# Work carried across three stage borders in a four-layer fp32 model on one Trainium2 core

## The chip, the core and the metric

The kernel runs on one core of one Trainium2 chip. A core has five engines with a queue of instructions each, which they work off in order: PE multiplies matrices (its weight loads are shown as PEld), DVE is the vector engine, ACT the scalar engine, POOL the third general engine, and SP only issues transfers. They meet at semaphores. The metric is the device time of one execution in microseconds (us), lower is better.

## The reference, cut to what matters

x is fp32, 16 sequences of 256 rows of 128 features. Four layers follow, each of two sublayers of one form:

```python
x = x + _layernorm(_L0_attn_ref(_layernorm(x), ...))     # causal attention
x = x + _layernorm(_L0_ffn_ref(_layernorm(x), ...))      # gated mlp
x = x + _layernorm(_L1_attn_ref(_layernorm(x), ...))     # a transformer of depth 4
x = x + _layernorm(_L1_ffn_ref(_layernorm(x), ...))      # soft mixture of experts
x = x + _layernorm(_L2_attn_ref(_layernorm(x), ...))     # causal attention
...                                                      # three more sublayers

def _layernorm(x, axis=-1, eps=1e-05):
    m = jnp.mean(x, axis=axis, keepdims=True)
    v = jnp.var(x, axis=axis, keepdims=True)
    return (x - m) / jnp.sqrt(v + eps)
```

The transformer and the soft mixture, whose borders the change touches:

```python
for i in range(DEPTH):                                   # _L1_attn_ref, DEPTH = 4
    x = x + self_attention(layer_norm(x, ln1_g[i], ln1_b[i]), Wq[i], Wk[i], Wv[i], Wo[i], bo[i])
    h = layer_norm(x, ln2_g[i], ln2_b[i])
    x = x + (jax.nn.gelu(h @ W1[i] + b1[i], approximate=False) @ W2[i] + b2[i])

logits = jnp.einsum('bmd,dnp->bmnp', x, phi)             # _L1_ffn_ref, n = 64, p = 32
dispatch = jax.nn.softmax(logits, axis=0)                # over the sequences b
combine = jax.nn.softmax(logits.reshape(bsz, m, n * p), axis=-1).reshape(bsz, m, n, p)
slots = jnp.einsum('bmd,bmnp->bnpd', x, dispatch)
y = jnp.einsum('bnpd,nde->bnpe', slots, W) + b[None, :, None, :]
out = jnp.einsum('bnpd,bmnp->bmd', y, combine)
```

## The kernel before, in words

x lies in on-chip memory as eight groups of four tiles, a tile being 128 rows of 128 features. A group is the unit of nearly all work: one instruction for a 128x512 block or four for its tiles. The stages follow one another, each with its own pools of buffers: L0 (attention and mlp), the transformer (l1a), the soft mixture (l1f), the second attention (l2a), a trunk, and the rest.

A layernorm is split over the engines. `stats` takes four bn_stats and four bn_aggr on DVE (lines 255 and 257), then `rsqrt` does a scale and a pow on POOL (L244, L245); `normed` writes four tiles on DVE (L264). Two functions inside L0 do the same with ACT: a second pair of small POOL operations (L577, L578) makes a bias, and four activations (L583) write the tiles. Before a matmul by features, four PE transposes by the identity (L306) go to a PSUM bank that ACT copies out.

Three stages matter, and the places where they touch.

L0. `group(g)` is a generator; `turns` steps the eight groups through the instruction order in a manual schedule, group g starting at turn 4g. A group ends with y = mlp output (L719), the normalisation of y and its addition to x (L724), and the normalisation of x into z[g], the transformer's input.

Transformer. `stage_l1_attn` first sets up buffers by memsets on POOL (L746, L748), two casts on DVE (L753), then runs 64 steps: in each of the four layers, eight `l1_mix` (attention, one per group) and eight `ffn`, of which up to five are interleaved. Each begins with `l1_norm_T`: stats, normed, transposes, and xT with the layer's gain and bias on ACT (L776). `l1_mix` has the matmuls wq, wk and tok. In the last layer each ffn adds its result to z (L794), normalises it and adds it to x (`residual`), and `fill` writes x to DRAM as xs (L958) and its normed form to mxn (L264), the mixture's input. The order within the pools is left to a scheduler, apart from the manual schedules of L0 and l2a.

Soft mixture. The slots are cut into eight blocks. `logits(n)` makes block n's logits (PE matmuls phi x mxT, copies lg on ACT, maxima mpart on DVE, L1010), `slots(n)` does the dispatch weights (DVE, L1031 to L1048) and the experts, `share(n)` adds the block's part to x: exponentials, transposes, matmuls my x meT, and on DVE x = x * fade + part (L1145). A loop steps share(n), logits(n + 2) and slots(n + 1) in turn. Ahead of it POOL makes a bf16 split of the experts' biases (L990 to L997). In the last block, after every second sequence, `end(g)` divides group g by its sum (L1164 to L1168), normalises it, and adds back the x that was saved in xs (L1170). The share waits for end(g) to be stepped through.

Second attention. `attention_stage` runs `head(0)` up to its fourth step, sets up buffers by POOL memsets (L344, L349), finishes head 0, and then `turns` the other heads and two batches a group; `beside`, which starts at turn 9, is here `l3_decays`, a set of small operations for the later trunk: 20 on DVE in one piece (L1266 and on), then 16 heads, one after another. Matmuls km x qT give the scores, and DVE takes their maximum (at_nm, L440).

Of the kernel before, what the change touches and what calls it, by code (L numbers as in the profile page):

```python
# [199 lines left out]
class Ctx:  # L200
# [61 lines left out]
    def normed(self, out, src, mv, rs):  # L262
        for k in range(NT):
            self.nc.vector.tensor_scalar(  # L264
                out[:, k, :], src[:, k, :], mv[:, k, 0:1], rs[:, k : k + 1], ALU.subtract, ALU.mult
            )

    def norm_to(self, out, src, wait=1):
# [272 lines left out]
        return out  # L541


def stage_l0(k, x, w, wv, wi, z):


    nc, v, gp = k.nc, k.nc.vector, k.nc.gpsimd
# [8 lines left out]
    def constants():  # L556
# [12 lines left out]
        for name in f:  # L569
            v.tensor_scalar(f[name], wi[name], float(np.float32(1.0 / 127.0)), None, ALU.mult)  # L570
            yield

    def stats(src):

        mv, rs = k.stats(src)
        nb = k.t([P, NT], "ln_nb", 6)
        gp.tensor_scalar(nb, mv[:, :, 0], -1.0, None, ALU.mult)  # L577
        gp.tensor_tensor(nb, nb, rs, ALU.mult)  # L578
        return nb, rs

    def normed(out, src, nb, rs):
        for t in range(NT):
            nc.scalar.activation(  # L583
                out[:, t, :], src[:, t, :], AF.Identity, bias=nb[:, t : t + 1], scale=rs[:, t : t + 1]
            )

    def by_feature(src, tag):
        ps = k.transposed_ps(src)
# [57 lines left out]
        v.tensor_tensor(to, ps[:, : 2 * D].rearrange("p (t d) -> p t d", t=2), bc(sm, 2, D), ALU.mult)  # L646

    def group(g):
        nb, rs = stats(x[g])
        yield from idle(2)  # L650
        xn = k.t([P, NT, D], "xn", 2)
        normed(xn, x[g], nb, rs)
        yield
        xT = by_feature(xn, "xT")
        yield
        qk = []
        for name in ("wq", "wk"):
            ps = k.ps("s")
            k.mm(ps[:32, :], w[name], xT)
            t = k.t([32, GT], name + "T", 2)  # L660
            nc.scalar.copy(t, ps[:32, :])
            qk.append(t)
        yield
        s0 = scores(qk, 0)
        ps = k.tokens_ps(xT, wfull)
        val = k.t([P, NT, D], "v", 3)
        nc.scalar.copy(val, ps)
        yield
        got0 = masked(s0)
        s1 = scores(qk, 1)  # L670
        yield
        e0, sm0 = weights(*got0)
        got1 = masked(s1)
        yield
        e1, sm1 = weights(*got1)
        eT0 = weights_T(e0)
        yield
        o0 = product(eT0, val, 0)
        eT1 = weights_T(e1)
        yield  # L680
        o = k.t([P, NT, D], "o", 3)
        divided(o, o0, sm0, 0)
        o1 = product(eT1, val, 1)
        yield
        divided(o, o1, sm1, 1)
        mv, rs = k.stats(o)
        yield from idle(2)
        k.normed(o, o, mv, rs)
        gp.tensor_tensor(x[g], x[g], o, ALU.add)
        yield  # L690
        nb, rs = stats(x[g])
        yield from idle(2)
        xn = k.t([P, NT, D], "xf", 2)
        normed(xn, x[g], nb, rs)
        yield
        xT = by_feature(xn, "xfT")
        yield
        h = k.t([P, 3, GT], "h", 2)
        todo = []
        for cs in ((0, 1), (2,)):  # L700
            for c, u, sg in todo:
                v.tensor_tensor(h[:, c, :], u, sg, ALU.mult)
            todo = []
            for c in cs:
                cols = slice(c * P, (c + 1) * P)
                gt = k.ps("s")
                k.mm(gt, f["gate"][:, cols], xT)
                u = k.ps("s")
                k.mm(u, f["up"][:, cols], xT)
                sg = k.t([P, GT], "sg", 4)  # L710
                nc.scalar.activation(sg, gt, AF.Silu)
                todo.append((c, u, sg))
            yield
        for c, u, sg in todo:
            v.tensor_tensor(h[:, c, :], u, sg, ALU.mult)
        yield
        ps = k.tokens_ps(h, down)
        y = k.t([P, NT, D], "y", 3)
        nc.scalar.copy(y, ps)  # L719
        yield  # L720
        mv, rs = k.stats(y)
        yield from idle(2)
        k.normed(y, y, mv, rs)
        gp.tensor_tensor(x[g], x[g], y, ALU.add)  # L724
        yield
        nb, rs = stats(x[g])
        yield from idle(2)
        normed(z[g], x[g], nb, rs)
        yield

    with k.tc.manual_schedule():
        k.turns([(0, group(0)), (0, constants())] + [(4 * g, group(g)) for g in range(1, NG)])


def stage_l1_attn(k, x, ws, rows, z, then):

    nc = k.nc

# [4 lines left out]
    k.l1_ctx = [k.t([P, 4, 68], f"l1_ctx{i}", 1) for i in range(2)]  # L743
    k.l1_max = [k.t([P, 2, 3, 4, 32], f"l1_max{i}", 1) for i in range(2)]
    for a in k.l1_val + k.l1_lin:
        nc.gpsimd.memset(a, 1.0)  # L746
    for a in k.l1_max + k.l1_ctx:
        nc.gpsimd.memset(a, 0.0)  # L748
    for a in k.l1_ctx:
# [3 lines left out]
        nc.vector.tensor_copy(a, k.c[n])  # L753

    def ffn(i, g):
        yield from l1_ffn(k, z[g], ws[i], rows[f"b2{i}"])
        if i == 3:
            yield
            yield from k.residual(x[g], z[g])
            yield  # L760
            yield from then(g)

    steps, leads = [], []
    for i in range(4):
        steps += [l1_mix(k, z[g], ws[i], rows[f"bo{i}"], NG * i + g) for g in range(NG)]
        steps += [ffn(i, g) for g in range(NG)]
        leads += [4] * NG + [2] * NG
    k.interleave(steps, 5, leads, -1)


# [6 lines left out]
    return out  # L777


def l1_ffn(k, z, w, b2):  # L780

    hT = yield from l1_norm_T(k, z, w["ln2_g"], w["ln2_b"])
    k.nc.gpsimd.tensor_tensor(z, z, bc(b2, 1, NT), ALU.add)
# [7 lines left out]
            yield  # L791
    ps = k.tokens_ps(h, w["w2"].rearrange("p (c n) -> p c n", c=4))
    yield
    k.nc.vector.tensor_tensor(z, ps, z, ALU.add)  # L794


def l1_mix(k, z, w, bo, n):


    nc, v = k.nc, k.nc.vector  # L800
# [1 line left out]
    val, lin, ctx, mx = k.l1_val[n % 3], k.l1_lin[n % 3], k.l1_ctx[n % 2], k.l1_max[n % 2]  # L802
    heads = [slice(32 * h, 32 * h + 32) for h in range(4)]
    tiles = lambda b: [slice((2 * b + t) * P, (2 * b + t + 1) * P) for t in range(2)]
    hT = yield from l1_norm_T(k, z, w["ln1_g"], w["ln1_b"])
    nc.gpsimd.tensor_tensor(z, z, bc(bo, 1, NT), ALU.add)
    yield

# [143 lines left out]
def soft_inputs(k, x, pool):  # L952

    xs = k.dram.tile([P, NG, NT, D], F32, tag="xs", name="xs")
    xn = [pool.tile([P, NT, D], F32, tag=f"mxn{g}", name=f"mxn{g}") for g in range(NG)]

    def fill(g):
        k.nc.sync.dma_start(out=xs[:, g], in_=x[g])  # L958
        yield from k.norm_to(xn[g], x[g])

    return xs, xn, fill


def stage_soft_moe(k, x, w, wdram, bdram, xn, xs):

# [15 lines left out]
    fade, less = {}, {}  # L983
    quarter = k.t([P, P], "mquarter", 1, dt=BF16)
    v.tensor_copy(quarter, w["quarter"])


    bias = k.t([P, 16 * D], "mbias", 1, dt=BF16)
    left = k.t([P, 16 * D], "mdisp", 3)
    nc.gpsimd.memset(left, 0.0)  # L990
    for i in range(3):
        nc.sync.dma_start(out=left[32 * i : 32 * i + 4, :], in_=bdram)
    nc.gpsimd.tensor_copy(bias, left)
    for i in (1, 2):
        for at in (slice(32, 64), slice(64, P))[i - 1 :]:
            nc.gpsimd.tensor_tensor(left[at, :], left[at, :], bias[at, :], ALU.subtract)
            nc.gpsimd.tensor_copy(bias[at, :], left[at, :])  # L997

    def logits(n):
        lg = lgs[n % 2]  # L1000
# [121 lines left out]
    def share(n):  # L1122
# [3 lines left out]
        for b in range(NB):  # L1126
# [15 lines left out]
            for t in range(2):  # L1142
# [3 lines left out]
                else:  # L1146
                    v.tensor_copy(x[g][:, at, :], ps[:, t, 0:D])
            nc.scalar.copy(got[:, :, b], ps[:, :, D])  # L1148
            yield
            if n == blocks - 1 and b % 2:  # L1150
                yield from end(b // 2, f, got)
        if n == 0:
            v.tensor_copy(sums, got)
        elif n < blocks - 1:
# [2 lines left out]

    def end(g, f, got):

        back = k.t([P, NT, D], "slT", 3)  # L1160
        nc.sync.dma_start(out=back, in_=xs[:, g])
        bs = slice(2 * g, 2 * g + 2)
        r = k.t([P, 2, 2], "mend", 2)
        v.tensor_tensor(r, sums[:, :, bs], f[:, :, bs], ALU.mult)  # L1164
        v.tensor_tensor(r, r, got[:, :, bs], ALU.add)
        v.reciprocal(r, r)
        xg = x[g].rearrange("p (b t) d -> p b t d", b=2)
        v.tensor_tensor(xg, xg, bc(r.rearrange("p t b -> p b t"), 3, D), ALU.mult)  # L1168
        n = yield from k.norm(x[g], "mdisp", 3)
        nc.gpsimd.tensor_tensor(x[g], back, n, ALU.add)  # L1170

    for n in range(-2, blocks):
        parts = [
# [1 line left out]
            logits(n + 2) if n + 2 < blocks else None,  # L1175
            slots(n + 1) if 0 <= n + 1 < blocks else None,
        ]
        parts = [p for p in parts if p]
        while parts:
            parts = [p for p in parts if next(p, k) is not k]  # L1180


def stage_l2_attn(k, x, w, beside):

    nc, v = k.nc, k.nc.vector

    def head(g, got):
        yield
        xn = yield from k.norm(x[g], "xn", 1, 2)
        yield  # L1190
        ps = k.transposed_ps(xn)
        xT = k.t([P, GT], "xT", 2)
        nc.scalar.copy(xT, ps)
# [26 lines left out]
        yield  # L1220
        yield from k.residual(x[g], y, 2)

    k.attention_stage(head, 10, 4, tail, beside)


def l2_ffn(k, x, w, b2):
# [598 lines left out]
def program(ctx: ExitStack, tc: tile.TileContext, xin, dram, at, out):  # L1825
# [44 lines left out]
    k.load = load  # L1870
    k.mhalf = base.tile([P, P], F32, tag="mhalf", name="mhalf")
    nc.gpsimd.memset(k.mhalf, -0.5)
    rows1 = load_rows(base, "l1rows")

    @contextmanager
# [12 lines left out]
    k.dram = ctx.enter_context(tc.tile_pool(name="spill", bufs=1, space=bass.MemoryType.DRAM))  # L1888
    pz = opened("z", "left")
    z = [pz.tile([P, NT, D], F32, tag=f"z{g}", name=f"z{g}") for g in range(NG)]  # L1890
    stage("l0", "left", stage_l0, l0, l0v, l0f, z, banks=ONE_RING)
    closed("w0")
    l2 = load(opened("wb", "right"), "l2")
    psoft = opened("soft", "right")
    l1f = load(psoft, "l1f")
    xs, xn, fill = soft_inputs(k, x, psoft)
    stage("l1a", "left", stage_l1_attn, l1, rows1, z, fill, banks=RING_BANKS)
    closed("z")
    closed("wa")

    stage("l1f", "left", stage_soft_moe, l1f, dram["l1fw"], dram["l1fb"], xn, xs)
    closed("soft")
    pe = opened("we", "right")
    last = load(pe, "l3", {"afc", "aproj"})
# [3 lines left out]
    rows3 = load_rows(pc, "l3rows")  # L1908
    pl = opened("lm", "right")
    lm = pl.tile([P, 16, SEQ + P], F32, tag="lm", name="lm")  # L1910
    stage("l2a", "left", stage_l2_attn, l2, l3_decays(k, rows3, lm, pl), banks=RING_BANKS)

    pm = opened("xm", "left")
    xm = [pm.tile([P, NT, D], F32, tag=f"xm_{g}", name=f"xm_{g}") for g in range(NG)]
# [39 lines left out]
```

## Time and profile before

| what | value |
|---|---|
| median of 3 runs | 2999.88 us (2999.87 to 3004.17) |
| profiled execution | 3001.28 us, of which span 2999.6 |
| busy | PE 92%, PEld 63%, DVE 65%, ACT 55%, POOL 34% |
| mean granted PE clock | 0.961 of full |
| last f_down matmul of L0, first transpose of the transformer | 172.6 us, 190.2 us |
| last mlp_h matmul, first phi matmul | 951.1 us, 968.5 us |
| last share matmul, first km,qT matmul | 1544.1 us, 1571.0 us |

Three views are used. The page lists busy time by engine, and the span in 40 slices with the busy share in tenths. The timeline lists instructions in order: start, duration, engine, line, operation, output and inputs, and in square brackets how long the engine was idle before and what ended that. The table by stage gives, for a chosen stretch, how long each engine was busy in it and the mean granted PE clock.

### The profile page before, as it was taken

The page shows a single profiled execution, that of the slowest core. Times are in us where ns is not written, and L with a number is a line of the kernel's source. Part 1 is how long each engine was busy: PE and PEld are TensorE (multiplying, and loading weights), DVE is VectorE, ACT ScalarE, POOL GpSimd, SP SyncE. Part 2 cuts the span into 40 slices and gives each one's busy share as a digit, 9 for nine tenths or more (in the row PEclk, how much of TensorE's full clock was granted, in tenths as well). Part 3 has the DMA queues.
Part 4 walks back from the last instruction along what each step waited for, and adds up shares of the span by engine and source line. Part 5 has one row for each costly group of instructions (what it writes and reads, how often), then busy time and mean ns, then how long its engine had stood idle before and what let it go on. Part 6 is the DMA issues. An engine that isn't in the chain of part 4 may idle for free.

```text
span 2999.6 us, 59389 instructions
## 1 busy us (share of the span) xinstructions
PE 2756.1 (92%) x23674; PEld 1881.2 (63%) x23674; DVE 1950.2 (65%) x5342; ACT 1661.9 (55%) x3488; POOL 1017.0 (34%) x1368
## 2 busy tenths in 40 slices
PE   8979999999997799999959998799999699978998
PEld 4547776777666588888843443466666344436897
DVE  5767466564667889999867775566674587735441
ACT  6745556455563667776725665344444277756543
POOL 3453333333335200000044555322231466644332
PEclk9989999999998899999979999899999799988999
DMA  4000000000001000000020000000000000010000
GB/s 115 12 1 2 1 2 2 1 2 1 2 2 37 1 12 12 8 9 9 9 73 1 1 1 1 1 1 1 1 1 1 2 1 1 1 42 16 2 15 15
DMA packets 29149, 31.29 MB, mean 10 GB/s; under 512 B 7292, under 2 KB 20156, under 8 KB 28732
## 3 DMA queue, kind: packets, MB, share of 16 engines
q1 hardware_dynamic: 28872, 27.49, 3.1%
q8 instruction: 187, 3.06, 0.4%
q14 instruction: 90, 0.74, 0.1%
HBM read 23.29 MB, written 4.19 MB: 9 GB/s over the span
## 4 chain that ended last, share of the span: by engine, by line
PE 51%; ACT 7%; DVE 6%; POOL 2%; issue 2%; DMA 0%; POOLq 0%; SPq 0%; ACTq 0%; DVEq 0%
PE ps_s L317 32%; PE ps_o L317 7%; PE ps_mm L317 6%; ACT at_e L472 1%; PE ps_s L306 1%; ACT lg L1129 1%; PE ps_xin L317 1%; ACT meT L1136 1%; PE ps_sum L317 1%; ACT mdisp L1036 1%; ACT lg L1009 1%; PE ps_s L506 1%; PE ps_t L1134 1%; DVE at_nm L440 1%; POOL ln_rs L245 1%
## 5 line engine op out<-in xcount | busy, mean ns | idle before, releaser
L244 POOL TENSOR_SCALAR ln_rs<-ln_mv 128x4 f32<-128x4 f32 x192 | 41.2, 215 | 879.6 <-DVE ln_mv L257 855.1
L440 DVE TENSOR_REDUCE at_nm<-ps_s 128x2 f32<-128x512 f32 (+1 forms) x384 | 238.1, 682 | 123.0 <-PE ps_s L317 123.0
L472 ACT ACTIVATE at_e<-ps_s 128x512 f32<-128x512 f32 x384 | 198.2, 603 | 93.3 <-PE ps_s L317 91.1
L1391 DVE TENSOR_TENSOR scan<-ps_s,lm 128x384 f32<-128x384 f32 x256 | 124.7, 549 | 143.1 <-PE ps_s L317 142.9
L478 POOL TENSOR_SCALAR_AFFINE_SELECT at_e<-at_e 128x1024 f32<-128x1024 f32 (+1 forms) x96 | 135.4, 1411 | 215.0 <-ACT at_e L472 214.7
L245 POOL TENSOR_TENSOR ln_rs<-ln_rs,mhalf 128x4 f32<-128x4 f32 x192 | 196.4, 1023 | 15.7
L854 DVE TENSOR_REDUCE l_max<-ps_s 128x3 f32<-128x384 f32 x256 | 124.1, 548 | 64.0 <-PE ps_s L317 64.0
L317 PE MATMUL ps_o<-my,meT 128*128 128x129 f32 x1024 | 145.6, 290 | 18.3 <-ACT mgot L1148 15.3
L317 PEld LDWEIGHTS ps_s<-l_w,mlp_h 128*128 128x128 f32 x1280 | 149.4, 192 | 18.8 <-issue 15.1
L317 PE MATMUL ps_s<-l1f_phi,mxT 128*128 128x256 f32 x512 | 141.5, 399 | 16.9 <-DVE mpart L1010 16.8
L317 PEld LDWEIGHTS ps_o<-my,meT 128*128 128x128 f32 x1024 | 128.8, 196 | 37.0 <-ACT mgot L1148 21.8
L317 PE MATMUL ps_s<-km,qT 32*128 32x512 f32 x768 | 140.0, 663 | 12.0 <-POOL km L364 10.5
L317 PE MATMUL ps_s<-l_w,mlp_h 128*128 128x128 f32 x1280 | 150.2, 275 | 0.3
L317 PE MATMUL ps_s<-qm,kT 32*128 32x512 f32 x768 | 144.2, 656 | 5.2 <-DVE at_nm L440 5.0
L904 POOL TENSOR_SCALAR_AFFINE_SELECT e<-e 128x512 f32<-128x512 f32 x128 | 78.8, 637 | 178.3 <-ACT e L901 178.3
L317 PE MATMUL ps_o<-at_e,at_vm 128*32 128x128 f32 (+1 forms) x2048 | 122.6, 336 | 15.3 <-ACT at_oT L502 15.3
L317 PE MATMUL ps_mm<-mdisp,mxn 128*128 128x128 f32 x1024 | 125.2, 278 | 5.0 <-DVE mdisp L1048 4.9
L901 ACT ACTIVATE e<-ps_s 128x384 f32<-128x384 f32 x256 | 105.5, 510 | 39.7 <-PE ps_s L317 39.6
L317 PEld LDWEIGHTS ps_mm<-mdisp,mxn 128*128 128x128 f32 x1024 | 121.6, 194 | 7.9 <-DVE mdisp L1048 6.6
L1368 ACT COPY BT<-ps_s 128x512 f32<-128x512 f32 x64 | 37.5, 586 | 154.6 <-PE ps_s L317 154.6
L317 PE MATMUL ps_s<-xT,l_w 128*128 128x512 f32 x256 | 119.3, 596 | 2.7 <-ACT mlp_h L789 2.7
L317 PEld LDWEIGHTS <-b_ident 128*128 128x128 bf16 x656 | 51.5, 98 | 110.0 <-issue 100.2
(427 smaller groups left out, 7083.9 us busy)
## 6 DMA issues: line engine op xcount, KB each, us to landing
mw<-in_l1fw SPq DMA_DIRECT2D x16, 256.0 KB, 2.7
moe_w<-in_moe SPq DMA_DIRECT2D x16, 256.0 KB, 5.3
l_w<-in_l SPq DMA_DIRECT2D x10, 256.0 KB, 3.4
x<-in_x SPq DMA_DIRECT2D x8, 256.0 KB, 4.6
xs<-x SPq DMA_DIRECT2D x8, 256.0 KB, 2.0
slT<-xs SPq DMA_DIRECT2D x8, 256.0 KB, 2.7
out<-x SPq DMA_DIRECT2D x8, 256.0 KB, 2.3
l1f_phi<-in_l1f SPq DMA_DIRECT2D x1, 1024.0 KB, 4.9
```

Of the source, the lines that this page charges most:

```text
L244: g.tensor_scalar(out, in_, scale, eps, ALU.mult, ALU.add)
L245: g.tensor_tensor(out, out, self.mhalf[:, :n], ALU.pow)
L306: self.nc.tensor.transpose(out[:n, k * P : (k + 1) * P], src[:, k, cols], self.c["ident"])
L317: self.nc.tensor.matmul(out, lhsT=lhsT, rhs=rhs, start=start, stop=stop, skip_group_check=True)
L440: v_.tensor_reduce(nm[:, t, r, vs], s, AX.X, ALU.max, negate=True)
L472: nc.scalar.activation(e[:, r], s, AF.Exp)
L478: nc.gpsimd.affine_select(at, at, [[0, 4], [0, n], [1, P]], ALU.is_ge, 0.0, base=0, channel_multiplier=-1)
L854: v.tensor_reduce(mx[:, b, :, h, 16], s, AX.X, ALU.max, negate=True)
L901: nc.scalar.activation(e[:, h].rearrange("p j n -> p (j n)"), s[:, : 3 * P], AF.Exp)
L904: nc.gpsimd.affine_select(e[:, :, j, :], e[:, :, j, :], [[0, 4], [1, P]], ALU.is_ge, 0.0, base=0, channel_multiplier=-1)
L1368: nc.scalar.copy(s, ps)
L1391: v.tensor_tensor(m, s[:, : SEQ + P], lm[:, SCAN_HEADS[4 * (t // 2) + 2 * i + hh], :], ALU.mult)
```

## The change

Work is carried from one stage into the next at three borders.

1. L0 into the transformer. Group 7 of L0 stops once y is copied to a buffer that outlives the stage (`hand_y`); its normalisation, the addition to x and z[7] follow as `rest_of_l0`, stepped beside the transformer's first mix. Group 0 of L0 goes further: it normalises z[0], transposes it and writes the first mix's input with that layer's gain and bias (`hand_xT`), so `l1_mix` for group 0 of layer 0 begins at its matmuls. The six memsets of l_val and l_lin go from POOL to DVE.
2. Transformer into the mixture. `fill` writes mxn on ACT and no longer on DVE (a new `stats_nb` and `normed_act`, the two functions of L0 made general). In the last layer the ffn of groups 6 and 7 (the keys of `k.over`) writes its result to xn[g], and its normalisation, the addition to x, xs and mxn follow as `late(g)`, stepped beside the logits of the first block. The biases' split is issued one iteration later.
3. Mixture into the second attention. `end` becomes a part of the loop of its own, and the share no longer steps through it. The division by the sum is no longer written to x: `soft_end` folds its reciprocal rt into the scale, rs = rt * (var * rt * rt + eps) ^ -1/2, by three more 128x4 multiplications on POOL, normalises x in place on DVE and adds the saved x. For groups 6 and 7 the last share leaves only rt; their `soft_end` runs in l2a, in `beside`, ahead of the decays. Group 0's statistics for l2a are taken right after its end and kept, and head 0 normalises on ACT.

```diff
+    def stats_nb(self, src, kept=None):
+        mv, rs = self.stats(src)
+        g = self.nc.gpsimd
+        nb, to = kept or (self.t([P, NT], "ln_nb", 6), rs)
+        g.tensor_scalar(nb, mv[:, :, 0], -1.0, None, ALU.mult)
+        g.tensor_tensor(nb, nb, rs, ALU.mult)
+        if kept:
+            g.tensor_copy(to, rs)
+        return nb, to
...
 def group(g):                                   # L0
-        y = k.t([P, NT, D], "y", 3)
+        y = y7 if g == NG - 1 else k.t([P, NT, D], "y", 3)
         nc.scalar.copy(y, ps)
         yield
+        if g == NG - 1:
+            return
...
+        if g == 0:
+            nb, rs = k.stats_nb(z[g])
+            yield from idle(2)
+            xn = k.t([P, NT, D], "xf", 2)
+            k.normed_act(xn, z[g], nb, rs)
+            yield
+            ps = k.transposed_ps(xn)
+            nc.scalar.activation(xT0, ps, AF.Identity, bias=l1["ln1_b"], scale=l1["ln1_g"])
+            yield
...
+def rest_of_l0(k, x, z, y):
+    yield from k.residual(x, y)
+    yield
+    nb, rs = k.stats_nb(x)
+    yield
+    k.normed_act(z, x, nb, rs)
...
     for a in k.l1_val + k.l1_lin:
-        nc.gpsimd.memset(a, 1.0)
+        nc.vector.memset(a, 1.0)
...
     def ffn(i, g):
-        yield from l1_ffn(k, z[g], ws[i], rows[f"b2{i}"])
-        if i == 3:
+        late = i == 3 and g in k.over
+        yield from l1_ffn(k, z[g], ws[i], rows[f"b2{i}"], xn[g] if late else z[g])
+        if i == 3 and not late:
...
+    steps[0] = beside(steps[0], rest_of_l0(k, x[NG - 1], z[NG - 1], y7))
...
     def fill(g):
         k.nc.sync.dma_start(out=xs[:, g], in_=x[g])
-        yield from k.norm_to(xn[g], x[g])
+        nb, rs = k.stats_nb(x[g])
+        yield
+        k.normed_act(xn[g], x[g], nb, rs)
...
+def soft_end(k, x, xs, rt, back):
+    v, gp = k.nc.vector, k.nc.gpsimd
+    k.nc.sync.dma_start(out=back, in_=xs)
...
+    rs = k.t([P, NT], "ln_rs", 6)
+    gp.tensor_tensor(rs, mv[:, :, 1], rt, ALU.mult)
+    gp.tensor_tensor(rs, rs, rt, ALU.mult)
+    k.rsqrt(rs, rs, 1.0, LN_EPS)
+    gp.tensor_tensor(rs, rs, rt, ALU.mult)
+    yield from idle(2)
+    k.normed(x, x, mv, rs)
+    gp.tensor_tensor(x, back, x, ALU.add)
...
+    def late(g):
+        y = k.t([P, NT, D], "slT", 3)
+        yield from k.norm_to(y, xn[g])
+        nc.gpsimd.tensor_tensor(x[g], x[g], y, ALU.add)
+        yield
+        yield from fill(g)
...
+            if n == blocks - 1 and b % 2:
+                parts.append(end(b // 2, f, got))
             yield
-            if n == blocks - 1 and b % 2:
-                yield from end(b // 2, f, got)
...
     def end(g, f, got):
-        v.reciprocal(r, r)
-        xg = x[g].rearrange("p (b t) d -> p b t d", b=2)
-        v.tensor_tensor(xg, xg, bc(r.rearrange("p t b -> p b t"), 3, D), ALU.mult)
-        n = yield from k.norm(x[g], "mdisp", 3)
-        nc.gpsimd.tensor_tensor(x[g], back, n, ALU.add)
+        rt = k.over[g] if g in k.over else k.t([P, NT], "mendt", 3)
+        v.reciprocal(rt.rearrange("p (b t) -> p t b", b=2), r)
+        if g in k.over:
+            return
+        back = k.t([P, NT, D], "slT", 3)
+        yield from soft_end(k, x[g], xs[:, g], rt, back)
+        yield
+        if g == 0:
+            k.stats_nb(x[g], k.kept)
...
+        if n == -2:
+            parts += [late(g) for g in k.over]
+        elif n == -1:
+            biases()
...
-def stage_l2_attn(k, x, w, beside):
+def stage_l2_attn(k, x, w, xs, decays):
+    def beside():
+        for g, rt in k.over.items():
+            yield from soft_end(k, x[g], xs[:, g], rt, k.t([P, NT, D], "back", 1))
+            yield
+        yield from decays
...
+        if g == 0:
+            xn = k.t([P, NT, D], "xn", 1)
+            k.normed_act(xn, x[g], *k.kept)
+            yield from idle(3)
+        else:
+            xn = yield from k.norm(x[g], "xn", 1, 2)
+            yield
```

## The prediction

> **What bounds the kernel now.** I read the page first: busy time of each engine and the slices.
>
> ```profile
> PE 2756.1 (92%) x23674; PEld 1881.2 (63%) x23674; DVE 1950.2 (65%) x5342; ACT 1661.9 (55%) x3488; POOL 1017.0 (34%) x1368
> PE   8979999999997799999959998799999699978998
> PEclk9989999999998899999979999899999799988999
> ```
>
> TensorE (PE) carries the kernel; time is to be had only where its digit falls. A slice is 75 us: the two 7s at slices 13 and 14 are the border into the soft mixture, the 5 at slice 21 the border into the second attention, the 7 at slice 3 the border into the transformer. The timelines of these places show why.
>
> Border 1, after the last f_down matmul at 172.6 us:
>
> ```profile
> 172.61 0.59 ACT L719 COPY y<-ps_s 128x512 f32<-128x512 f32 x1 [3.32 <-PE ps_s L317]
> 181.44 1.65 ACT L583 ACTIVATE z<-x,ln_nb,ln_rs 128x128 f32<-128x128 f32 x4 [5.95 <-POOL ln_nb L578]
> 188.65 3.13 POOL L245 TENSOR_TENSOR ln_rs<-ln_rs,mhalf 128x4 f32<-128x4 f32 x3
> 190.22 1.15 PE L306 MATMUL ps_s<-const_ident,xn 128*128 128x128 f32 x4 [17.64 <-DVE xn L264]
> 195.86 1.49 PE L317 MATMUL ps_s<-l_tok,xT 128*128 128x256 f32 x3
> ```
>
> Group 7's two normalisations (y, then z) end at 183.1, then the first groups' statistics, a queue of POOL memsets and three pow (L245) pass before PE gets xn. The tok matmuls of the first mixes start at 195.9, 207.3, 222.2 and 238.2, and then every 15.9: from the third on, PE is the pacer (15.69 busy of 15.9 in the table by stage).
>
> Border 2, after the last mlp_h matmul at 951.1, from the timeline and the table by stage (columns: stretch, length, busy PE, PEld, DVE, ACT, POOL, granted clock, DMA share, GB/s):
>
> ```profile
> 961.55 2.05 DVE L264 TENSOR_SCALAR mxn<-x,ln_mv,ln_rs 128x128 f32<-128x128 f32 x4 [0.25 <-POOL ln_rs L245]
> 966.08 1.11 DVE L264 TENSOR_SCALAR mxn<-x,ln_mv,ln_rs 128x128 f32<-128x128 f32 x4 [1.42 <-POOL ln_rs L245]
> 968.49 2.04 PE L317 MATMUL ps_s<-l1f_phi,mxT 128*128 128x256 f32 x4
> ```
>
> ```profile
> 957.60:968.50 10.90, 2.41 (x10) 1.80 (x10) 8.35 (x38) 0.59 (x1) 5.88 (x10) 0.50 0.09 29
> 968.50:983.40 14.90, 14.90 (x68) 11.74 (x67) 8.14 (x13) 7.32 (x13) 10.35 (x4) 0.87 0.13 41
> 983.40:991.60 8.20, 6.94 (x26) 4.06 (x24) 4.76 (x8) 3.77 (x7) 8.00 (x4) 1.00 0.01 2
> 991.60:1040.80 49.20, 32.29 (x205) 24.19 (x206) 48.08 (x63) 28.90 (x48) 3.20 (x2) 0.83 0.00 0
> ```
>
> VectorE (DVE) has fallen behind: its z additions (L794) come 6.6 us apart (943.65, 950.28, 956.90) because each group costs 0.68 + 1.23 + 1.20 + 1.11 + 2.05, and all must pass before phi starts. Then DVE is idle for some 10 us (logits of block 0), and from 991.6 it is full: 48.08 of 49.20.
>
> Border 3, the last share in the chain of waits, then head 0 of the attention in the timeline:
>
> ```profile
> 1539.22 0.85 DVE mdisp L264 x3
> 1540.72 1.24 DVE x L1168
> 1542.22 0.78 DVE ln_st L255 x4
> 1543.65 1.03 POOL ln_rs L245
> 1544.97 0.85 DVE mdisp L264 x3
> ```
>
> ```profile
> 1558.58 1.80 POOL L344 MEMSET at_vm<- 128x2048 f32 x1
> 1562.49 1.03 POOL L245 TENSOR_TENSOR ln_rs<-ln_rs,mhalf 128x4 f32<-128x4 f32 x1
> 1564.35 1.09 PE L306 MATMUL ps_s<-const_ident,xn 128*128 128x128 f32 x4 [19.79 <-DVE xn L264]
> 1570.96 1.14 PE L317 MATMUL ps_s<-km,qT 32*128 32x512 f32 x8
> ```
>
> The chain repeats every 5.75 us a group: DVE normalises, scales (L1168), takes statistics, waits for POOL. The last share matmul starts at 1544.1, km,qT only at 1570.96: 26.8 us.
>
> **The change part by part.** Everything is summed against the profiled 3001.28 us (span 2999.6 and 1.7 around it), 1.4 above the median 2999.88; the forecast goes from the median.
>
> Border 1. Out of the path: the end of group 7 (172.6 to 183.1) and the preparation of group 0 (to 192.3, first wq); stats, normed, transposes and xT of group 0 move into L0, their ACT (1.65 + 0.78), DVE (1.2), POOL (1.65) and PE (1.15) lying beside group 7's work; there I charge 1.9 for the last f_down being pushed. wq then follows the last f_down, and from wq to tok took 3.6 (192.29 to 195.86): tok comes at 172.6 + 1.9 + 3.6 = 178, 18 earlier. But groups 1 and 2 are no longer prepared while PE idles: the second mix needs its own stats, pow, normed, transposes and xT behind six memsets now on DVE (2.4 by POOL's rows, 1.60 + 0.82), two casts (1.2) and rest_of_l0's two stats and normed (3.5). The distance of the first mixes lies between the steady 15.9 and 22.3 (15.7 of PE plus 6.6 unprepared front: 1.1 + 1.15 + 0.78 + 3.6); I take 18, nearer the steady row. Fourth mix: 178 + 3 x 18 = 232 against 238.2: **-6**, with -12.5 and +6.7 as the ends.
>
> Clock: PE stopped at 172.6, the granted clock fell at 177.2 and was back at 197.6, 7.4 us after PE resumed; 6.5 busy us of that ran at half, so 3.2 are at stake. The Trainium skill (TensorE: Matmul & The Clock Gate, Part 1) says that a clock is lost after an idle window of about 3.4 us and regained after as long a busy one. By the rule, a border without such a gap keeps the clock, and I could add 3 us here and 2 at border 3. But the trace lost the clock at 1535.6 (0.66 from 1535 to 1537, then 0.50) when no PE gap since 1515 had passed 1.6 us and PE was 63% busy. A border filled with small gaps can thus still be halved: I take nothing for the clock; the rule's sum would be 5 lower.
>
> Border 2. fill's normed goes to ACT (4 x 0.41 = 1.65 a group) and leaves DVE (1.1 to 2.05), so DVE's 6.6 a group falls under PE's 5.3 and the backlog goes. Groups 6 and 7 need only 0.68 before phi. Phi comes at about 951.1 + 0.7 + 0.6 (mxT) + transposes = 953.8, 14.7 earlier. ACT pays: four more instructions ahead of the last mlp_h, **+1.8**. Inside logits of block 0, late(6) and late(7) put 2 x (1.23 + 1.11 + 1.2) = 7.1 us on DVE, and eight ACT normed (3.3), waiting for POOL's pow, ahead of lg copies; DVE had 12.9 busy of 23.1 there, so about half shows: +4. The bias chain (1.89 + 8.22 + 3.83 + 4.06 + 2.77 = 20.8 on POOL) now stands behind late's POOL work (about 8), its third DMA behind the xs writes on SP's queue; it ends some 31 us after phi's start, still 32 ahead of its first reader at 1031.4 - 968.5 = 63. But it then lies beside the DVE-full dispatch:
>
> ```profile
> 993.03 1.88 DVE L1014 TENSOR_TENSOR mtop<-mtop,mpart 128x32 f32<-128x32 f32 x1
> ```
>
> This costs 0.18 elsewhere; here it ended with POOL's cast (992.09 + 2.77). The row gives two such holds, 2.1 us. The Trainium skill (SBUF — State Buffer, Who interferes with whom) says that a DVE instruction with two SBUF inputs is blocked for the whole of a POOL instruction that reads SBUF; by it the chain's last three instructions could each hold DVE, 4.1 + 2.8 + 2. I take the row, +2; the rule's sum is 6 higher. Border 2: -14.7 + 4 + 2 + 1.8 = **-7**, ends -14 and +1.
>
> Border 3. In the share tail L1168 (1.24) goes; POOL gains three 128x4 products of 0.20 each (row L578's 0.20; the pow L245, 1.02, is the other end), which lie under the fourth x update of 0.26 to 0.34 and the 1.1 wait. 5.75 becomes 4.5 for four paced groups, **-5** (at 1.02 each, +5). Groups 6 and 7 leave no norm in the tail. After the last share matmul POOL still has one addition (about 3 us on), the at_vm and at_pc memsets (5.7) and km (1.9): km,qT after about 11 instead of 26.8; head 0's normed (ACT 1.65) is covered by these. **-15.5**. Given back: soft_end of 6 and 7 adds 4.6 us of DVE and 6.2 of POOL, and two loads of back, among the first at_nm; today's similar burst of decays opens a gap of 5.0 (1589.4 to 1594.5). I take +2 (0 to 6). The decays start eight turns of about 3 us later; today they end at 1859.9, 10 us before PE's stop at 1870.7, so about two heads (each ACT 0.5, POOL 0.87, DVE 0.42 and waits) fall behind the attention: +3.5 (0 to 9). Border 3: **-15**.
>
> Sum: -6 - 7 - 15 = -28 (2973 in the profiled execution): 2999.9 - 28 = **2972**.
>
> **The rivals.**
> A, given back: only the waits ahead of the first matmuls go, and each stage's pacer (DVE at 991 to 1050, the mixes behind unprepared groups, at_nm behind soft_end) takes them back. For it: DVE is 48.08 of 49.20 full there. Against: at border 3 PE is full from 1594 on. Then border 1 gives -2, border 2 0, border 3 -6: 2992.
> B, more: the clock stays whole and no lock holds DVE: -28 - 5 - 2 - 4 = -39, 2961.
> C, slower: one mechanism, DVE's queue held at soft_end's in-place normed. DVE works in order; each soft_end puts a normed there that needs POOL's chain of six, and POOL may be at a 1.9 km or a 2.0 mask. With 5 us of hold in each of eight groups (the decays' gap), -28 + 40 = +12: 3012. It is slower than before from 28 / 8 = 3.5 us, and measurably so from (28 + 6) / 8 = 4.2 us a group; against it, today's same wait is 1.1 and idle(2) spaces the two.
> D: no visible change, if A's gains and the late decays cancel: 2998.
>
> **How the numbers follow.** Forecast 0.58, A 0.20, B 0.08, C 0.08, D 0.06. A change under 0.2% (6 us) can't be told from none here. Faster is forecast, A and B: 0.86; same 0.06; slower 0.08. The range goes from between B and the forecast to A: 2955 to 2992.
>
> **What would show it.** Right: no PE gap over 4 us at 172 to 185; first tok about 178, fourth about 232; phi within 4 us of the last mlp_h; share groups 4.5 apart; km,qT about 11 after the last share matmul. Wrong: L1016's product near 1 us; second mix over 20 behind the first; dispatch TENSOR_TENSORs held by mbias casts; PE gaps in the second attention ended by DVE x (soft_end); a gap over 12 us ahead of the trunk.

## The result and the profile after

The changed kernel took 2974.82 us in the median of 4 runs (2974.3 to 2976.73) beside 3000.74 for the kernel before; the ratio is 0.9913, its 95% interval 0.9896 to 0.993, and 26 us are gained where 28 were forecast. The profiled execution took 2974.3, its span 2972.5. The page after:

```profile
PE 2756.0 (93%) x23673; PEld 1878.9 (63%) x23674; DVE 1930.3 (65%) x5300; ACT 1675.4 (56%) x3528; POOL 1020.9 (34%) x1407
PE   8889999999998799999978997899999699978998
```

PE does the same 2756 us of work; the 7 at slice 3 and one 7 at slice 13 became 8, the 5 at slice 21 a 7. A slice moves with the kernel's length, so the other digits that differ are not read here. Laid side by side, the timelines of the two kernels give the table below. All times are starts in us (172.6 and 951.1, given further up for the kernel before, are the ends of the same matmuls), and the last column is after minus before; it adds up from row to row, so what one border gives is the difference to the row above it.

| place | before | after | |
|---|---|---|---|
| last f_down matmul | 172.3 | 171.3 | -1.0 |
| tok of mix 1, 2, 3, 4 | 195.9, 207.3, 222.2, 238.2 | 174.0, 195.8, 214.6, 229.9 | -21.8, -11.6, -7.6, -8.2 |
| last mlp_h matmul | 950.8 | 944.6 | -6.2 |
| first phi | 968.5 | 948.0 | -20.5 |
| first dispatch tensor_tensor | 991.5 | 976.4 | -15.1 |
| share of block 0 | 1040.8 | 1026.5 | -14.3 |
| first, last matmul of share 7 | 1491.5, 1544.1 | 1477.0, 1527.6 | -14.6, -16.5 |
| first km,qT, and the 73rd | 1571.0, 1612.8 | 1539.4, 1586.8 | -31.5, -26.0 |
| first transpose of the trunk | 1879.6 | 1855.0 | -24.6 |
| end of the span | 2999.6 | 2972.5 | -27.1 |

Two readings of this table need care. L0's end wanders from profile to profile (169.3 to 173.8 over all kernels here), so a border is measured from a neighbouring stage. And from the trunk on, where no kernel was changed, the profile of before is longer than every other: 1120.0 us from the trunk's first transpose to the end, against 1117.5 after and 1116.1 to 1118.0 in the twelve other kernels. In that stretch PE worked 71.2 us at half clock (granted clock 0.50) in before and 62.7 to 66.2 us in the others; half of the difference is 2.5 to 4.3 us, about what before takes longer. So the clock accounts for it (see below); it was no part of the forecast.

Border 1, timeline:

```profile
172.21 1.12 PE L336 MATMUL ps_s<-hand_xT,l_wq 128*128 128x512 f32 x2 [0.68 <-ACT hand_y L725]
174.03 1.89 PE L336 MATMUL ps_s<-l_tok,hand_xT 128*128 128x256 f32 x8
189.25 0.45 PE L325 MATMUL ps_s<-const_ident,xn 128*128 128x128 f32 x1 [2.06 <-DVE xn L264]
```

The gap of 17.64 is one of 0.68. But the second mix's transposes wait for DVE, whose queue held memsets, casts, rest_of_l0 and the first mix's maxima ahead of xn; its tok comes 21.7 after the first. This is read from the order in the timeline; no run here takes these parts of the queue away one by one.

Border 2, timeline:

```profile
948.01 1.97 PE L336 MATMUL ps_s<-l1f_phi,mxT 128*128 128x256 f32 x8 [1.23 <-POOL mdisp L1052]
957.88 3.78 PE L336 MATMUL ps_s<-l1f_phi,mxT 128*128 128x256 f32 x8 [3.39 <-DVE mxT L237]
957.51 1.65 ACT L283 ACTIVATE mxn<-x,ln_nb,ln_rs 128x128 f32<-128x128 f32 x4 [3.74 <-POOL ln_nb L275]
976.41 2.17 DVE L1101 TENSOR_TENSOR mdisp<-lg 128x1024 f32<-128x1024 f32 x1
978.50 1.87 DVE L1084 TENSOR_TENSOR mtop<-mtop,mpart 128x32 f32<-128x32 f32 x1
```

Phi follows 3.4 us after the last mlp_h matmul. Then PE waits for an mxT copy that stands behind late's statistics on DVE, ACT waits for POOL's chain ahead of the lg copies, and from first phi to first dispatch it takes 28.4 instead of 23.0. The last two lines are the first dispatch work, held by POOL's bias split. (An instruction is called held where it lasts longer than the same one elsewhere while POOL works beside it; these two take 1.21 and 0.18 elsewhere.)

Border 3, share tail and first scores, timeline:

```profile
1517.29 1.26 POOL L1021 TENSOR_TENSOR x<-slT,x 128x512 f32<-128x512 f32 x1 [1.23 <-DVE mend L1233]
1517.41 1.17 DVE L1234 TENSOR_TENSOR mend<-mend,mgot 128x4 f32<-128x4 f32 x1
1521.82 1.12 DVE L264 TENSOR_SCALAR x<-x,ln_mv,ln_rs 128x128 f32<-128x128 f32 x4 [1.31 <-POOL ln_rs L1018]
1561.18 2.09 PE L336 MATMUL ps_s<-km,qT 32*128 32x512 f32 x8 [2.14 <-POOL km L383]
1574.27 1.91 DVE L1355 TENSOR_SCALAR sp_u<-sp_e 128x16 f32<-128x16 f32 x1 [0.39 <-ACT sp_e L1353]
1583.33 1.22 PE L336 MATMUL ps_s<-qm,kT 32*128 32x512 f32 x1 [7.55 <-DVE at_nm L459]
```

The tail still takes 5.72 us a group (normed at 1516.10, 1521.82): L1168 is gone, but a 128x4 sum that mostly took 0.15 before now takes 1.17, until POOL's addition ends. The timeline of before had shown the exchange in one of its groups, where L1165, the same sum, was held and L1168 was not; the next L1165 took 0.15 and the next L1168 1.32:

```profile
1522.42 1.12 DVE L1165 TENSOR_TENSOR mend<-mend,mgot 128x4 f32<-128x4 f32 x1
1524.04 0.68 DVE L1168 TENSOR_TENSOR x<-x,mend 128x512 f32<-128x512 f32 x1
```

km,qT starts 11.8 after the last share matmul instead of 26.8. Then the decays' burst leaves PE idle for 7.55, where it was 5.03 before:

```profile
1594.48 1.21 PE L317 MATMUL ps_s<-qm,kT 32*128 32x512 f32 x1 [5.03 <-DVE at_nm L440]
```

### The profile page after: what moved, and what is told of

It reads as the page before. It is cut to its first block, busy times and chain, and to the rows that moved or that the text cites. A ratio compares the mean times of both kernels' runs of the same rounds, so it can differ in the third digit from the quotient of the medians.

```text
span 2972.5 us, 59427 instructions
## 1 busy us (share of the span) xinstructions
PE 2756.0 (93%) x23673; PEld 1878.9 (63%) x23674; DVE 1930.3 (65%) x5300; ACT 1675.4 (56%) x3528; POOL 1020.9 (34%) x1407
## 4 chain that ended last, share of the span: by engine, by line
PE 51%; ACT 7%; DVE 6%; POOL 2%; issue 2%; POOLq 0%; ACTq 0%; DVEq 0%
PE ps_s L336 32%; PE ps_o L336 7%; PE ps_mm L336 6%; ACT at_e L491 1%; PE ps_s L325 1%; ACT lg L1199 1%; PE ps_xin L336 1%; ACT meT L1206 1%; PE ps_sum L336 1%; ACT mdisp L1106 1%; ACT lg L1079 1%; PE ps_t L1204 1%; DVE at_nm L459 1%; PE ps_s L525 1%; POOL ln_rs L245 1%
## 5 line engine op out<-in xcount | busy, mean ns | idle before, releaser
L336 PEld LDWEIGHTS ps_s<-l_w,mlp_h 128*128 128x128 f32 x1280 | 149.5, 192 | 19.8 <-issue 15.1
L336 PE MATMUL ps_s<-l1f_phi,mxT 128*128 128x256 f32 x512 | 141.8, 401 | 21.5 <-DVE mpart L1080 15.7
L941 POOL TENSOR_SCALAR_AFFINE_SELECT e<-e 128x512 f32<-128x512 f32 x128 | 78.6, 635 | 172.9 <-ACT e L938 172.9
```

Of the source, the lines that this page charges most:

```text
L336: self.nc.tensor.matmul(out, lhsT=lhsT, rhs=rhs, start=start, stop=stop, skip_group_check=True)
L941: nc.gpsimd.affine_select(e[:, :, j, :], e[:, :, j, :], [[0, 4], [1, P]], ALU.is_ge, 0.0, base=0, channel_multiplier=-1)
```

## The experiments

The kernels no_over, decays_first, late_spread, no_late and bias_short rest on two runs each, the other kernels on four or more.

**One border at a time.** Each kernel has one border's edits and the other two as before.

b1_alone: 

> The first border's change alone, the other two as before. If the borders are independent, it gives what the two traces show there, -8 us (from the fourth mix on: 238.2 to 229.9), and keeps it to the end: 2992. If a later stage's pacer takes gains back (VectorE at 991 to 1050), less than half of it is left at the end: over 2996.

b2_alone: 

> The second border's change alone. Independent: -6 (phi 12 us earlier after the last mlp_h and the fill on ACT +2, then the logits of block 0 give back 6): 2994. If the logits' loss of 6 us comes from the first border's shift and not from late(g), the loss is absent here and it gives -12: 2988.

b3_alone: 

> The third border's change alone. Independent: -12 to -13 (tail -2, start -15, first scores +6, then -2): 2987. If the trunk's 2 us belong to chance of the clock, -10: 2990.

Ratios: 0.9972 (0.9962 to 0.9982), 0.9966 (0.9953 to 0.9979), 0.9948 (0.9933 to 0.9963); medians 2992.88, 2991.62 and 2986.32 beside 3001.45. Their product is 0.9887, a larger gain than the change's 0.9913 and outside its interval of 0.9896 to 0.993; b2 and b3 gained more by the run times than expected. The profiles let one leave out L0's end and the trunk: from the last f_down matmul to the trunk's first transpose, before took 1707.3 and the three 1700.9 (-6.4), 1703.2 (-4.1) and 1693.1 (-14.2), together -24.7; the change took 1683.8, -23.5. So the sum holds to about a microsecond, with one profile of each. The parts hold less well: inside the change's profile they are -7.2 (to the fourth tok), -6.0 (to the share of block 0) and -10.3, so b3 alone gave 4 more than the third border does in the change; 3 of these are the clock's (see below). Most of what is lost of a border's first gain is lost inside that border. b1's fourth mix came 6.1 earlier; that the change's own profile shows 2 more is L0's wandering end. b2 shows the loss in the logits without border 1 (first phi -15.5, share of block 0 -9.0), so border 1 does not cause it.

**The share tail.** mend_psum forms the sum from the PSUM bank (the memory that PE writes to) in one-column pieces, and in the last block leaves out ACT's copies to got, for which no DVE instruction of the steady tail had waited:

```diff
-        v.tensor_tensor(r, sums[:, :, bs], f[:, :, bs], ALU.mult)
-        v.tensor_tensor(r, r, got[:, :, bs], ALU.add)
+                for t in range(2):     # in the share, for each sequence b of the last block
+                    v.scalar_tensor_tensor(
+                        r[:, t, b % 2 : b % 2 + 1], sums[:, t, b : b + 1], f[:, t, b : b + 1],
+                        ps[:, t, D : D + 1], ALU.mult, ALU.add
+                    )
```

> The changed kernel, but the sum of the share tail is formed by one-column scalar_tensor_tensor reads of the PSUM result (four a group, as the x updates, one SBUF input each) and no longer by two 128x4 tensor_tensors of two SBUF inputs. If the tail's 5.72 us a group is kept by VectorE being held for POOL's addition (L1234 1.17 instead of 0.15), a group falls to about 4.8 and the kernel by 4 us against the change: 2971. If POOL's chain of six is what paces the tail, nothing moves: 2975.

Its timeline:

```profile
1518.29 1.11 DVE L264 TENSOR_SCALAR x<-x,ln_mv,ln_rs 128x128 f32<-128x128 f32 x4 [0.84 <-POOL ln_rs L1018]
1519.48 1.27 POOL L1021 TENSOR_TENSOR x<-slT,x 128x512 f32<-128x512 f32 x1 [1.23 <-DVE x L264]
1522.88 1.12 DVE L264 TENSOR_SCALAR x<-x,ln_mv,ln_rs 128x128 f32<-128x128 f32 x4 [0.85 <-POOL ln_rs L1018]
1529.09 0.34 DVE L1224 SCALAR_TENSOR_TENSOR mend<-sums,mfade,ps_o 128x1 f32<-128x1 f32 x2
```

A steady group takes 4.59, and share 7 runs from 1479.3 to 1526.9: 47.6 instead of 50.7. POOL's chain stands in the loop in both kernels and takes the same time from its first product to its last (1519.65 to 1521.78 in the change, 1520.71 to 1522.85 here). What shrank is DVE's part ahead of it, by the hold: the chain alone was not the pacer. In the steady groups the new reads come after the addition; at 1529.09 they ran beside one (1528.67 to 1529.93) and took 0.34 for two. The kernel's median is 2973.01 (ratio 0.9905, 0.9889 to 0.9922), 2 below the change and not separable from it by run times.

**The groups ended in the next stage.** no_over ends groups 6 and 7 inside the share:

```diff
-        rt = k.over[g] if g in k.over else k.t([P, NT], "mendt", 3)
+        rt = k.t([P, NT], "mendt", 3)
-        if g in k.over:
-            return
 # and in l2a, beside():
-        for g, rt in k.over.items():
-            yield from soft_end(k, x[g], xs[:, g], rt, k.t([P, NT, D], "back", 1))
-            yield
```

> The changed kernel, but groups 6 and 7 of the mixture are ended inside their stage as the other groups are. Each then costs a tail period (5.7 us) ahead of head 0's matmuls as far as POOL's memsets wait behind them, and the first scores lose the two soft_ends: km,qT 9 to 11 us later after the last share matmul, 3 us less lost from there to the 72nd: slower than the change by 6 to 8. If the two soft_ends are the cause of the 5.5 us, it is level with the change.

2979.96 (ratio 0.9933, 0.9913 to 0.9953). km,qT starts 21.9 after the last share matmul (change: 11.8), and from there to the 73rd it takes 41.3 instead of 47.3; the gap of 2.14 is gone and the decays' gap is 5.03 again. So the 5.5 us that the change gives back there all come with the two soft_ends, some 3 of them by way of the clock (see below); carrying them over is still worth 4 net at that point, and 5 in the run.

**The decays' burst.** decays_first issues its first part ahead of head 0's end:

```diff
+    next(decays)
     k.attention_stage(head, 10, 4, tail, beside())
```

> The changed kernel, with the first part of the decays (the burst of small VectorE operations) issued ahead of head 0's end, where VectorE waits. If the burst (4.8 us, and 3.5 of holds by POOL) is what PE's gap of 7.55 us stands for, the gap is gone, the half clock behind it too, and the kernel gains 8 to 10: 2966. If soft_end's normed and km's wait behind POOL are the larger part of the 5.5 us given back at the first scores, 2 to 3 are won. Against either, qT may start up to 2 us later.

2965.11 (ratio 0.9883, 0.9863 to 0.9903). The first scores come 2.7 later relative to the last share matmul, because qT now stands behind the burst, and the 73rd km,qT 9.1 earlier. In between PE works 3.4 us at half clock where it was 9.3, so part of the gain is the clock's. The gap of 7.55 is not in the timeline, the other one is:

```profile
1542.67 1.51 PE L336 MATMUL ps_s<-km,qT 32*128 32x512 f32 x8 [2.44 <-DVE qT L1293]
1565.50 1.14 PE L336 MATMUL ps_s<-km,qT 32*128 32x512 f32 x8 [2.14 <-POOL km L383]
```

**The logits of block 0.** late_spread steps late(6) two steps and late(7) five steps later; no_late leaves out late's work except the write to xs; bias_short leaves out six of the seven instructions of the bias split (the low parts of the biases).

```diff
 # late_spread, in late(g)
+        yield from idle(2 if g == NG - 2 else 5)
 # no_late, in late(g)
-        y = k.t([P, NT, D], "slT", 3)
-        yield from k.norm_to(y, xn[g])
-        nc.gpsimd.tensor_tensor(x[g], x[g], y, ALU.add)
-        yield
-        yield from fill(g)
+        nc.sync.dma_start(out=xs[:, g], in_=x[g])
+        yield
 # bias_short, in biases()
-        for i in (1, 2):
-            for at in (slice(32, 64), slice(64, P))[i - 1 :]:
-                nc.gpsimd.tensor_tensor(left[at, :], left[at, :], bias[at, :], ALU.subtract)
-                nc.gpsimd.tensor_copy(bias[at, :], left[at, :])
```

> The changed kernel, with late(6) stepped two steps of the logits later and late(7) five, so that their statistics no longer stand in VectorE's queue ahead of the first mxT copies. If that queueing (PE idle 3.39 us before VectorE's mxT) and the wait of ACT's normed make the 5.4 us that the logits of block 0 lost, from first phi to first dispatch tensor_tensor it takes 23 to 25 us instead of 28.4, and the kernel gains 4. If the bias split, which now ends later still, holds the dispatch instead (up to 4.1 us an instruction), the gain is eaten: 0 or slower.

> The changed kernel, leaving out the late ends of groups 6 and 7 ahead of the mixture (their normalisation, the addition to x and the normed input; only the write to xs is kept). If late's VectorE, ACT and POOL work inside the logits of block 0 is the 5.4 us lost there, first phi to first dispatch tensor_tensor takes 22 to 23 us instead of 28.4, and the bias split ends early enough to hold nothing: 7 to 8 faster than the change. If the clock or the logits' own ring is the cause, it stays above 26.

> The changed kernel, leaving out the bias split's low parts: POOL makes the first cast (1.9 us) and not the six instructions after it. If VectorE's first dispatch instructions are held by POOL's reads (L1101 2.17 and L1084 1.87 us), they take 1.2 and 0.2 and the dispatch starts 2.7 us earlier relative to the first phi; the stretch from first phi to it stays at 28.4. If they are slow for another reason, nothing moves.

no_late: 2968.78 (ratio 0.9897, 0.9877 to 0.9916). First phi to first dispatch is 21.5 us (947.82 to 969.33), 6.9 less than in the change, so late is the cause of the loss. (About 2 of the 6.9 may be the clock, which was whole there; in before and in the change PE worked 4.0 and 4.8 us of the stretch at half clock, so the loss of 5.4 between these two is not the clock's.) The second half of its expectation failed: the split still holds the dispatch (1.94 and 1.87), because the dispatch came earlier too, and the kernel is 6 below the change and not 7 to 8.

bias_short: 2973.63 (ratio 0.9913, 0.9893 to 0.9933). The stretch stays at 28.0 and the holds are gone, as its timeline shows; share of block 0 comes 2.6 earlier relative to the first phi. At the kernel's end the profile shows nothing left of it: from the 192nd km,qT to the trunk it took 187.8 instead of 183.8, with the same gaps of PE to 0.01 us, and PE worked 11.5 us at half clock there instead of 2.4. The 4 us go with the clock.

```profile
975.78 1.21 DVE L1097 TENSOR_TENSOR mdisp<-lg 128x1024 f32<-128x1024 f32 x1
976.91 0.18 DVE L1080 TENSOR_TENSOR mtop<-mtop,mpart 128x32 f32<-128x32 f32 x1
```

late_spread: 2978.25 (ratio 0.9927, 0.9907 to 0.9947), no gain; from first phi to first dispatch it took 35.0. POOL's bias split slipped in between late's own POOL work:

```profile
967.58 4.06 POOL L1058 TENSOR_TENSOR mdisp<-mdisp,mbias 64x2048 f32<-64x2048 f32 x1
972.49 1.64 PE L325 MATMUL ps_t<-const_ident,mxn 128*128 128x128 f32 x4 [6.29 <-ACT mxn L283]
```

ACT's normed of group 7 waited 5.99 for a pow and a 0.20 us product, each of which stood behind a 4.06 us instruction. The rival named in its expectation was right on the culprit, by another way: not DVE held, but POOL's queue.

**Together.** all_three has the sum from PSUM, the spread and the burst first; sum_and_decays leaves the spread out; sum_decays_shift also starts the soft_ends one turn later.

```diff
 # sum_decays_shift, in beside() of l2a
+        yield from idle(1)
         for g, rt in k.over.items():
```

> The sum formed from PSUM, the late groups spread, and the decays' burst first, together. If each acts in its own place, the gains add: -4 for the sum, -4, -8, so 2959 (2955 to 2966).

> The changed kernel with the sum formed from PSUM and the decays' burst first. The two lie at different places: -3 and -9.7 add to 2962 (2959 to 2965), faster than the change beyond its interval.

> As sum_and_decays, with the soft_ends in the attention begun one turn later, so that POOL meets head 1's km ahead of the chain of group 6 instead of behind it. If the 2.14 us that PE waits for km comes from the chain standing ahead of it, that gap goes and 2 us are won. If km waits for its own input, nothing moves.

2969.16 (0.9903, 0.9887 to 0.992), 2964.14 (0.9883, 0.9867 to 0.99) and 2963.63 (0.9879, 0.9864 to 0.9894). The first misses its 2959 by the spread's loss. The second can't be told from decays_first by its interval; the sum's 3 us are seen in its profile (share 7 takes 47.6) and not in the run times. In the third, PE's wait of 2.14 for km is gone from the timeline, so the order on POOL made it, and still nothing is won: its 192nd km,qT comes at 1660.5, against 1659.2. The second and third lie some 10 us below the change.

## Why the prediction was right, and where not

- **Border 1, -6.** Measured -6.1 at the fourth mix in b1_alone and -8.2 in the change's own profile. The first tok came 2.8 after the last f_down matmul's start, where the step's terms make 3.9: at 174.0 in the change and 176.3 in b1_alone, and not at 178. The fourth tok came 55.9 after the first, not 54. The terms were off by 2 to 4 in opposite directions, so that the -6 was met is in part luck. The distances are uneven (21.7, 18.9, 15.3): the first is the wait for DVE's queue, and over 20 was named as a sign of being wrong; 3 us of the second are the clock's (see below).
- **The charge of 1.9 on L0.** The last f_down matmul lies at 172.9 in the mean of the eleven kernels with border 1 changed and at 170.5 in the three without: 2.4. The two ranges overlap (171.3 to 173.8 and 169.3 to 172.3), so this is no more than agreement.
- **ACT ahead of the last mlp_h, +1.8.** Measured 1.7 (-7.9 at the last tok, -6.2 at the last mlp_h).
- **Phi 14.7 earlier.** Measured 14.3. **Logits, +4:** measured 5.4. **The lock, +2:** the two holds came to 2.65 against 2.11 before, so only 0.5 was new; the step forgot that the first dispatch instructions were held before as well. (Such holds were named as a sign of being wrong; they came.) By the rule of the Trainium skill (SBUF — State Buffer, Who interferes with whom) each of the chain's last three instructions could have held DVE; two did, with 0.96 and 1.69 (the sum by the rule, 4.1 + 2.8 + 2, is 7 above the row and not 6). The row was the better size. The sum of border 2, -7, met -6.0 in the change (from the fourth tok to the share of block 0), and -4.1 in b2_alone.
- **The share tail, -5: this step failed.** It took the 1.24 of L1168 off the period. The profile showed 0.68 for the same instruction at 1511.81 and 1524.04, so half of it was a hold by POOL's addition and belonged to the place, not to the instruction. With L1168 gone, L1234 stood there and was held for 1.17. Measured -1.9; the -3 that were missing came in mend_psum, whose reads take one of their two tensors from PSUM. The rule quoted at border 2 would have told it; the prediction did not use it here.
- **From share to km,qT, -15.5.** Measured -15.0 (11.8 for 11).
- **First scores, +2: mis-sized.** Measured +5.5 in the change and +2.3 in b3_alone; what lies between is the clock's (see below). The step took the decays' burst as equal on both sides. It now meets POOL's mask and qm work, which holds two of its small instructions (1.91 and 1.92; before, one of 1.49), and the gap grew from 5.03 to 7.55. That km waits behind soft_end's chain (2.14) costs nothing that shows: sum_decays_shift took the wait away and won nothing. Upper end given was 6.
- **Late decays, +3.5: mis-sized the other way.** From the 192nd km,qT to the trunk it cost 0.7.
- **The clock, 0: right to distrust the rule, wrong at nothing.** Nothing was taken for it, against the Trainium skill's rule (TensorE: Matmul & The Clock Gate, Part 1) of an idle window of some 3.4 us. The change's table by stage shows that the border without its gap did lose the clock:

```profile
176.00:181.00 5.00, 2.44 (x25) 1.38 (x25) 4.32 (x23) 1.99 (x5) 2.03 (x7) 1.00 0.01 3
181.00:187.00 6.00, 5.60 (x37) 3.92 (x37) 6.00 (x26) 2.43 (x10) 2.83 (x5) 0.51 0.00 0
200.00:215.00 15.00, 14.08 (x126) 9.04 (x127) 10.81 (x48) 6.17 (x19) 6.78 (x11) 0.77 0.01 3
1560.10:1566.90 6.80, 5.72 (x24) 1.65 (x27) 4.93 (x12) 0.83 (x2) 4.42 (x8) 0.50 0.11 37
```

The longest PE gap in the first two rows was 2.42 us, and the clock was halved just as PE was busy again. At border 3 it fell at 1515.7, twelve us ahead of the last share matmul, and was 0.50 until km,qT started. A halved clock can cost time only where PE works: around border 1 PE worked 18.1 us at half clock after the change and 6.5 before, though the halved time is the same (20.5 us). The mean granted clock does not tell this; it even rose, from 0.961 to 0.964.

How much that costs is seen where two kernels with the same code at a place ran it with another clock. In late_spread the rows that match the last two show a whole clock:

```profile
200.00:215.00 15.00, 14.27 (x154) 9.78 (x154) 11.24 (x44) 7.37 (x22) 6.75 (x10) 1.00 0.01 3
1565.70:1572.50 6.80, 5.80 (x40) 2.84 (x40) 5.70 (x17) 2.82 (x6) 4.84 (x11) 1.00 0.12 37
```

| stretch | clock whole, or nearly | clock halved for longer |
|---|---|---|
| second tok to third | 15.7 us in late_spread, no_late, bias_short, no_over | 18.9 in the change, b1_alone, mend_psum, sum_and_decays, sum_decays_shift |
| first km,qT to the 73rd | 44.2 in b3_alone, late_spread | 47.2 to 47.8 in the change, mend_psum, no_late, bias_short |

(In decays_first and all_three the clock was halved for 3.4 us between the two toks instead of 6.8, and it took 16.6 and 16.7.) So about 3 us of the third mix (2 over the first four, which take 53.7 or 55.8 to 55.9) and 3 of the 5.5 us at the first scores are the clock's. When a stretch is halved differs from kernel to kernel with the same code there; what decides it is not shown. No run here sets the clock on purpose: this rests on kernels that differ elsewhere.

The forecast's -28 was the sum of -6, -7 and -15. With one border at a time the profiles give -6.4, -4.1 and -14.2, and in the change -7.2, -6.0 and -10.3, up to the trunk; another 2.4 come behind it, where nothing was changed. That the total was met within 2 us is thus in part luck: the share tail and the first scores fell short by 3 and 3.5, the late decays were 3 too dear, and the trunk's 2.4 stood in no term. The range's lower end, 2955, lies below rival B (2961) and not between B and the forecast as it says. Rival A's idea, that the stages take gains back, holds at each border, but not in its size. Rival C's wait, DVE standing at soft_end's normed until POOL's chain is through, is 1.3 us in the tail and none in the attention; there one normed took 2.61 instead of 1.11 beside POOL's km product. That is 1.5 us, not the 4.2 it needed.

## What to carry to other kernels

The gain at a border is read from what the second and third unit of work wait for, not from the first: the first moved 21.8, 14.3 and 15.0 us against what lay ahead of it, and 6.4, 4.1 and 14.2 stayed with one border changed at a time. An instruction that is slow because another engine holds it does not take its slowness with it when removed; ask what will stand in its place. Before a burst of small instructions is passed over as "the same as before", look at what the change puts beside it: here its place was worth 10 us. Before a loss of some 3 us is put down to the code, look up how long PE worked at half clock in that stretch.

## What was not expected of the hardware

A DVE instruction of 4 elements a partition took 1.17 us instead of 0.15 beside a 1.26 us addition on POOL, and ones that read a PSUM operand in its stead were not held beside such an addition (two in 0.34). A normed of four tiles took 2.61 instead of 1.11 when POOL's km product (1.89) ran beside it. The PE clock was halved at 181 us after 5 us of 49% busy and no gap above 2.42. The same code took 15.7 or 18.9 us between two mixes, and 44.2 or 47.3 at the first scores, by when the clock was halved.
